# Values by the seven-product scheme, and two projection chains interleaved step by step, in a sandwich of attention and gated feed-forward

## The chip, the cores and the metric

The kernel runs on one core of a Trainium2 chip. The metric is the device time of one execution in microseconds (us); the time before is 1585.0 us, the median of three runs (1584.58 to 1585.37). One further execution was profiled. In the text TensorE is PE in the profile's letters (PEld is its weight load), VectorE is DVE, ScalarE is ACT, GpSimd is POOL and SyncE is SP, which here only issues transfers.

## The reference, cut to what matters

The input x has 8 batches of 512 rows of 256 numbers, in 32-bit floats. There are 16 heads of 64 numbers each.

```python
x = x + _layernorm(attention(_layernorm(x)))
x = x + _layernorm(feed_forward(_layernorm(x)))

# attention, per batch
q, k, v = x @ w_q, *split(x @ w_kv)          # 256 -> 1024 each, then 16 heads
q = l2norm(q) * exp(scale);  k = l2norm(k)   # per head and row
out = softmax(q k^T) v                       # 512 x 512 scores per head
return out @ w_out + b_out                   # 1024 -> 256

# feed-forward
h = silu((x @ w1) * s1) * ((x @ w2) * s2)    # 256 -> 1024
h = gelu((h @ h1) * hs1);  h = gelu((h @ h2) * hs2)   # 1024 -> 1024, weights -1, 0, 1
return (h @ w3) * s3                         # 1024 -> 256
```

## The kernel before, in words

The attention of all 8 batches runs first and the feed-forward of all 8 after it. Only the attention part is touched by the change; the feed-forward part starts when the last batch's attention is done.

**Units.** The attention goes by head pairs: a batch has 8 pairs, and a pair of a batch is a unit, so there are 64 units. Pairs 0 to 3 use the first half of the q, k and v columns (half 0, 512 columns), pairs 4 to 7 the second (half 1). A unit's own work is: `scores` (L738: eight products of 64 rows by 512, called s), the exponentials on ACT (L749, tile e, scaled by the key norms kn), their sum over the key blocks on DVE (`summed`, L772, tile es), `values` (L792: products of e with v, called po), the copy of po to oT on ACT (L888), and for every second unit the row sums pd on PE (L816) with their inverse: copied to d on ACT (L830), folded by an SP transfer (L858) to a small tile, inverted on DVE (L878), stored and spread by two more SP transfers (L864, L869), and multiplied into oT on DVE (L898).

**The order of the work.** PE does its work in the order in which the code adds it. For unit k that is: values of k, row sums, the work put in the odd slot 2k+1, scores of unit k+1, the work put in the even slot 2k, and then values of k+1. What is beside a unit is named in the table `BESIDE`, one string for each pair of a batch: c is one step of a query or key projection, v a step of the value projection, q and k the query and key norms (odd slot; all others even), m the key norms' transposes, o an output projection of 128 rows of the batch before, x the layer norm and transposes of the next batch's input, t the sums of token quarters, l a load. Steps of half 1 for the batch itself stand in the first strings, steps for the next batch in the later ones. The other engines and SP do their work in an order that a planner (`Steps.issue`) writes out beforehand from estimated costs; each engine and the SP queue then runs its list in that order, whatever the actual times are.

**The projections.** For batch 0 all projections are plain products (`qk_step`, `v_step`). For batches 1 to 7 queries and keys of a half go by a chain of seven products of quarters (Strassen's scheme in Winograd's form, `qk_chain`), L539: the weights are cut in four 128 by 256 quarters, the transposed input aT in four 128 by 256 quarters, sums of them are made on DVE (the weights' once, in `qk_weight_sums`, tile wsum; the input's once per batch in `token_sums`, tile tsum), and each product is two matmuls of 256 columns instead of the eight quarter products of the plain way. Products 1, 6, 7 and 4 are added up in one bank of PSUM (g1), products 5 and 3 in another (g2), product 2 in a third (g3). In between, ACT copies the intermediate sums out (`kept`, L560) or DVE adds them to what was kept (`added`, L570), and ACT squares the result for the norms (`squared`, L578). A product that adds to g1 has to wait until the sum before it is copied or added. The values go by the plain way in all batches: `v_step` is two matmuls of 512 columns (L407, tile vp) and one copy on ACT (L721), four steps for a half.

**The norms.** `norms_step` multiplies the squares with a matrix of ones (L627, pn), copies the sums on ACT to a tile nd (L651), and for queries folds them by SP (L633), inverts them on POOL, stores them (L674) and spreads them (L641, tile spread) for a multiplication into qT on DVE (L684). For keys `key_norms` transposes nd on PE (L698, pk) and POOL takes the power to kn. The tiles d and nd come from one pool of two buffers (`sqp`, tag "sq").

**PSUM.** Seven banks are dealt out in turn to all of this (`wbank`), an eighth holds po. A chain holds g1 and g2 over several steps.

**Weight work.** In the DVE's free time the kernel checks that the feed-forward weights are what the fast way presumes (`looked_at`: an SP load into tile w, L1083; `marked` L1090 and `gathered` L1095 on DVE, 512 columns each) and makes the sums of quarters of h1 and h2 (`weight_sums`, L1127, stored to DRAM by L1131). Tile w has two buffers.

Of the kernel before, what the change touches and what calls it, by code (L numbers as in the profile page):

```python
# [17 lines left out]
P = 128  # L18
# [121 lines left out]
def tile_fast(  # L140
# [143 lines left out]
    wp = attn_scope.enter_context(tc.tile_pool(name="wp", bufs=2))  # L284
# [115 lines left out]
    def projected(key, b, t, w, c0):  # L400
# [3 lines left out]
        def run():  # L404
# [11 lines left out]
            "pe", 1.72, run, reads=[(("aT", b), t)], writes=[(key, 0)],  # L416
# [55 lines left out]
    wsum = qksum.tile([P, 4, 3, 2 * P], F32, name="wsum")  # L472
    HS = S // 2

    def quarter(which, hf, k):
        w = wq_sb if which == "q" else wk_sb
        if k[0] == "A" or k == "S3":
            i, j = (1, 0) if k == "S3" else (int(k[1]) - 1, int(k[2]) - 1)
            return w[:, j, hf * HALF + i * HS : hf * HALF + (i + 1) * HS]
        return wsum[:, "qk".index(which) * 2 + hf, "S1 S2 S4".split().index(k), :]  # L480

    def qk_weight_sums(which, hf):
# [35 lines left out]
    def qk_chain(b, hf, which):  # L518
# [3 lines left out]
        to, sq, t = (which + "T", b, hf), ("spread", *n), ("tsum", b)  # L522
        g, tags = [("g1", *n), ("g2", *n), ("g3", *n)], {}

        def product(k, a, x, bank, fresh, last=False):
# [4 lines left out]
            def run():  # L530
# [7 lines left out]
                for o in range(2):  # L538
                    nc.tensor.matmul(  # L539
                        T[key][:, o, :], lhsT=w[:, ts(o, P)], rhs=rhs,  # L540
                        start=(fresh and o == 0), stop=True, skip_group_check=True,
                    )
# [10 lines left out]
        def part(i, k):  # L553
            return T[to][:, 2 * i : 2 * i + 2, ts(k, HS)]

        def kept(i, k, key, first=False):
            def run():
                if first:
                    tile_of(qkTp, [P, HP, S], which + "T", to)
# [4 lines left out]
                takes=[(which + "T", 2, to)] if first else (),  # L564
# [9 lines left out]
        def squared(i):  # L574
# [6 lines left out]

            steps.add(
# [14 lines left out]
        def fourth():  # L597
            added(0, 1, product(3, "S4", "B22", 1, False, last=True))

# [3 lines left out]
        def sixth():  # L603
            added(0, 0, product(2, "A12", "B21", 2, True, last=True))
            squared(0)
# [5 lines left out]
        return [first, second, third, fourth, sixth, fifth, seventh]  # L611
# [170 lines left out]
    def values(b, p, jb):  # L782
# [4 lines left out]
        def products():  # L787
# [13 lines left out]
            "pe", 0.86, products, reads=[(e, 0), (e, 1), (v, jb)], writes=[(po, 0)],  # L801
# [100 lines left out]
    def out_proj(b, t, pairs=(0, NP), tail=False):  # L902
# [72 lines left out]
        "c c v c c c c v c x x x x",  # L975
        "k o m o t",
        "c c o c c c c o c",
        "q v v l",
        "c c v c c c c v c",
        "k v",  # L980
        "c c m c c c c v c",
# [7 lines left out]
    def chains(b, hf):  # L989

        for w in "qk":
            yield from (lambda k=k, w=w: link(b, hf, w, k) for k in range(7))

    links = {}

    def link(b, hf, w, k):
        if k == 0:
            links[w] = qk_chain(b, hf, w)
# [9 lines left out]
    def beside():  # L1008
# [4 lines left out]
        c = [s for b, hf in c for s in ((b, s) for s in chains(b, hf))]  # L1013
        n = [(b, lambda b=b, hf=hf, w=w: norms_step(b, hf, w)) for b, hf in n for w in "qk"]
        m = [(b, lambda b=b, hf=hf: key_norms(b, hf)) for b, hf in m]
        v = [(b, lambda b=b, hf=hf, t=t: v_step(b, hf, t)) for b, hf in v for t in range(NT)]
        x = [(b, lambda b=b, t=t: norm_in(b, "a", t, ("xres", b))) for b in range(1, B) for t in range(NT)]
        o = [(b, lambda b=b, t=t: out_proj(b, t)) for b in range(B - 1) for t in range(NT)]
        for b in range(B):
            for p, some in enumerate(BESIDE):  # L1020
                for k in some.split():
                    later = p > 1 and (p > 3 or k in "cqkm")
# [12 lines left out]
                    elif (b + 1 < B) if later else b:  # L1035
                        yield b * NP + p, k, {"c": c, "q": n, "k": n, "m": m, "v": v}[k].pop(0)[1]
        assert not (c or n or m or v or x or o)
# [31 lines left out]
    loose = const.tile([P, S], I32, name="loose")  # L1069
# [7 lines left out]
    def looked_at(n, k, rows_of, after):  # L1077
# [3 lines left out]
        def load():  # L1081
            dst = tile_of(wp, [P, HID], "w", w)
            nc.sync.dma_start(  # L1083
                dst if len(rows_of.shape) == 2 else dst.rearrange("p (c n) -> p c n", n=D), rows_of
            )

        def marked(i):

            a, y = T[w][:, ts(i, S)], ("y", n, k, i)
            nc.vector.scalar_tensor_tensor(  # L1090
                tile_of(sump, [P, S], "y", y, bufs=1), a, 0.0, a, ALU.is_equal, ALU.add
            )

        def gathered(i):
# [6 lines left out]
            "sync", 0.1, load, lag=9.0, writes=[(w, 0), (w, 1)], takes=[("wrows", 2, w)], earliest=after  # L1101
        )
        for i in range(2):
            y = ("y", n, k, i)
            steps.add(
                "dve", 0.72, lambda i=i: marked(i), reads=[(w, i)], writes=[(y, 0)],
# [1134 lines left out]
```

## Time and profile before

| | |
|---|---|
| median of the runs | 1585.0 us |
| the profiled execution's own time | 1584.32 us |
| its span, first to last instruction | 1582.5 us |
| PE / DVE / ACT / POOL busy, share of the span | 99 / 67 / 58 / 31% |
| attention, until the last output projection | about 979 us |
| one batch of the attention in the middle (577.54 to 697.60 us) | 120.06 us |
| in it: PE / DVE / ACT / POOL busy | 120.06 / 62.22 / 69.67 / 26.58 us |
| granted TensorE clock, mean | 0.998 |

The shares say which engine is full, and the chain that ended last says whether the time follows from it. The table of a batch is read by stretches: each stretch shows the PE's busy time beside its length. A 32-bit matmul is shown as two records, so a chain product of two matmuls has four.

### The profile page before, as it was taken

What the parts mean: (1) busy time and instruction counts of PE and PEld (TensorE: products, weight loads), DVE (VectorE), ACT (ScalarE), POOL (GpSimd) and SP (SyncE); (2) the same over time, 40 slices, a digit from 0 to 9 for tenths busy, and PEclk for the clock granted to TensorE, in tenths of its full rate; (3) what the DMA queues carried; (4) which work ended last, traced back from release to release, by engine and by line L of the source; (5) the groups of instructions that cost most, each with busy time, mean ns of one, the idle gap of its engine ahead of it and who ended that gap; (6) DMA issues with size and microseconds to landing.
All of it is one profiled execution on the core that took longest, in us unless ns stands there. A gap on an engine that the chain in (4) does not pass through costs nothing.

```text
span 1582.5 us, 19689 instructions
## 1 busy us (share of the span) xinstructions
PE 1564.5 (99%) x7208; PEld 996.6 (63%) x7208; DVE 1059.5 (67%) x1772; ACT 917.6 (58%) x1543; POOL 486.6 (31%) x354
## 2 busy tenths in 40 slices
PE   9999999999999999999999999999999999999997
PEld 4344554554554554554554546788888888888886
DVE  4577776786654553554544557869877886879686
ACT  4666556556556556555555553666466636655662
POOL 4212122122221221321221211554165235625451
PEclk9999999999999999999999999999999999999999
DMA  6233433342220220220221313344324523451540
GB/s 178 65 97 102 120 82 109 121 115 76 54 62 15 58 65 15 58 62 18 58 64 43 85 38 88 111 142 156 121 80 133 171 69 107 146 152 49 160 133 29
DMA packets 77829, 142.66 MB, mean 90 GB/s; under 512 B 18844, under 2 KB 34460, under 8 KB 73628
## 3 DMA queue, kind: packets, MB, share of 16 engines
q1 hardware_dynamic: 58140, 78.40, 17.9%
q0 software_dynamic: 18880, 61.87, 12.5%
q8 instruction: 58, 0.95, 0.3%
q10 hardware_dynamic: 704, 1.05, 0.2%
q14 instruction: 47, 0.39, 0.1%
HBM read 123.49 MB, written 17.29 MB: 89 GB/s over the span
## 4 chain that ended last, share of the span: by engine, by line
PE 96%; DVE 2%; DMA 1%; ACT 0%; issue 0%; POOL 0%; SPq 0%; DVEq 0%
PE g L1494 26%; PE s L738 15%; PE po L792 14%; PE pa L914 7%; PE vp L407 7%; PE p L1420 6%; PE g_q L539 5%; PE g_k L539 5%; PE py L1608 4%; PE pd L816 2%; PE pn_q L627 1%; PE pn_k L627 1%; PE kp L433 1%; PE qp L433 1%; PE pk L698 0%; DMA spread_q<-nq 0%
## 5 line engine op out<-in xcount | busy, mean ns | idle before, releaser
L749 ACT ACTIVATE e<-s,kn 128x512 f32<-128x512 f32 x512 | 306.7, 702 | 96.6 <-PE s L738 96.6
L738 PE MATMUL s<-qT,kT 64*128 64x512 f32 x1024 | 237.1, 602 | 0.0
L1494 PE MATMUL g<-h,wb_S 128*128 128x512 f32 x1024 | 234.3, 389 | 0.0
L792 PE MATMUL po<-e,v 128*64 128x512 f32 x1024 | 233.9, 598 | 0.0
L1494 PEld LDWEIGHTS g<-h,wb_S 128*128 128x128 f32 x1024 | 192.0, 188 | 39.8
L738 PEld LDWEIGHTS s<-qT,kT 64*128 64x128 f32 x1024 | 93.6, 186 | 143.2 <-issue 125.7
L1494 PE MATMUL g<-h,wb_A 128*128 128x512 f32 x768 | 176.4, 389 | 0.0
L314 POOL TENSOR_TENSOR kn<-kn,neghalf 128x32 f32<-128x32 f32 x16 | 87.5, 5468 | 285.8 <-DVE kn L702 285.8
L772 DVE TENSOR_TENSOR es<-es,e 128x1024 f32<-128x1024 f32 x128 | 156.8, 1225 | 24.9 <-ACT e L749 14.0
L1494 PEld LDWEIGHTS g<-h,wb_A 128*128 128x128 f32 x768 | 144.0, 188 | 29.7
L792 PEld LDWEIGHTS po<-e,v 128*64 128x64 f32 x1024 | 69.4, 136 | 139.7 <-issue 131.1
L1312 DVE TENSOR_TENSOR h<-C,h 128x512 fp32r<-128x512 f32 x112 | 129.4, 1211 | 3.9 <-ACT h L1302 3.8
L314 POOL TENSOR_TENSOR nf_q<-nf_q,neghalf 128x32 f32<-128x32 f32 x16 | 87.3, 5456 | 144.9 <-DVE nf_q L661 144.9
L772 DVE TENSOR_TENSOR es<-e,e 128x1024 f32<-128x1024 f32 x64 | 78.3, 1224 | 72.2 <-ACT e L749 71.9
L1312 DVE TENSOR_TENSOR h<-B,h 128x512 fp32r<-128x512 f32 x112 | 107.8, 1001 | 27.1 <-ACT h L1302 26.7
L407 PE MATMUL vp<-wv_sb,aT 128*128 128x512 f32 x256 | 120.6, 599 | 0.0
L914 PE MATMUL pa<-wo_sb,oT 128*128 128x256 f32 x512 | 116.5, 381 | 0.0
L1550 POOL TENSOR_TENSOR B<-B,B 128x512 f32<-128x512 f32 x64 | 102.0, 1621 | 38.9 <-DVE B L1451 34.0
L914 PEld LDWEIGHTS pa<-wo_sb,oT 128*128 128x128 f32 x512 | 95.8, 190 | 20.0 <-ACT e L749 6.1
L888 ACT COPY oT<-po 128x512 f32<-128x512 f32 x64 | 37.4, 584 | 120.2 <-PE po L792 118.2
L878 DVE RECIPROCAL fold<-fold 128x16 f32<-128x16 f32 x31 | 7.8, 252 | 147.0 <-DMA fold<-d 147.0
L1550 POOL TENSOR_TENSOR C<-C,C 128x512 f32<-128x512 f32 x64 | 94.0, 1495 | 27.7 <-DVE h L1312 27.2
(170 smaller groups left out, 2320.8 us busy)
## 6 DMA issues: line engine op xcount, KB each, us to landing
wb_S<-s POOLq DMA_DIRECT2D x32, 1024.0 KB, 5.1
spread_q<-nq SPq DMA_DIRECT2D x32, 512.0 KB
rden<-r SPq DMA_DIRECT2D x62, 256.0 KB
wb_A<-in_h1T_dram POOLq DMA_DIRECT2D x12, 1024.0 KB, 5.6
wb_A<-in_h2T_dram POOLq DMA_DIRECT2D x12, 1024.0 KB, 5.6
s<-w SPq DMA_DIRECT2D x32, 256.0 KB
w<-in_h1T_dram SPq DMA_DIRECT2D x8, 512.0 KB
x<-xres SPq DMA_DIRECT2D x32, 128.0 KB
```

The costliest lines, as they stand in the source:

```text
L314: nc.gpsimd.tensor_tensor(d, d, neghalf.to_broadcast([P, n]), ALU.pow)
L407: nc.tensor.matmul(pm, lhsT=T["aT", b][:, c, ts(t, P)], rhs=w[:, c, c0 : c0 + HALF], start=(c == 0), stop=(c == ND - 1),)
L539: nc.tensor.matmul(T[key][:, o, :], lhsT=w[:, ts(o, P)], rhs=rhs, start=(fresh and o == 0), stop=True, skip_group_check=True,)
L738: nc.tensor.matmul(tile_of(ps_w, [P, S], tags[h], ss[h]), lhsT=T[kT][hp, j, ts(jb, P)], rhs=T[qT][hp, j, :], start=True, stop=True,)
L749: nc.scalar.activation(T[e][:, h, :], T[ss[h]], AF.Exp, scale=T["kn", b, hf][:, jb, 2 * j + h : 2 * j + h + 1],)
L772: nc.vector.tensor_tensor(T[t], T["e", b, p, 0] if jb == 1 else T[t], T["e", b, p, jb], ALU.add)
L792: nc.tensor.matmul(T[po][h * DH : (h + 1) * DH, :], lhsT=T[v][:, jb, c0 : c0 + DH], rhs=T[e][:, h, :], start=(jb == 0), stop=(jb == NT - 1),)
L914: nc.tensor.matmul(T[pm], lhsT=T["oT", b, p][:, ts(t, P)], rhs=wo_sb[:, p, :], start=(p == 0), stop=(p == NP - 1),)
L1312: lambda: nc.vector.tensor_tensor(T[h][:, 1, c, :], T[raw][:, c, :], T[h][:, 0, c, :], ALU.subtract),
L1420: nc.tensor.matmul(T[ps[k]], lhsT=(w1r, w2r)[k][c][:, ts(o, P)], rhs=row_halves(b, i)[0][:, c, :], start=(c == 0 and i == 0), stop=(c == N ...
L1494: nc.tensor.matmul(T[to[o]], lhsT=T[w][:, c, ts(o, P)], rhs=T[h][:, i, c, :], start=(first and c == 0 and i == 0), stop=(c == NQ - 1 and i ...
L1550: lambda: (nc.gpsimd if T_ENGINE == "pool" else nc.vector).tensor_tensor(T[dst][:, c, :], T[x][:, c, :], T[y][:, c, :], ALU.subtract),
```

## The change

The values of batches 1 to 7 go by the same chain of seven products as queries and keys: `qkv_chain` takes "v" too, with the input as the stationary and the weights as the moving operand, and squares nothing for it. Its weight sums are added (`qkv_weight_sums`, six groups instead of four), and they stand behind the value projections of batch 0 in the code, since one of them overwrites a quarter of the weights.

Two chains now run beside each other, a step of the one and a step of the other in turn. In the strings of `BESIDE`, c is a step of a query chain, d of a key chain, v of a value chain. Pair 0 has key and value chain of the batch's half 1, pair 2 query and key chain of the next batch's half 0 with two output projections among their first steps, pair 6 the query chain of half 1 and the value chain of half 0 of the next batch. Pairs 3, 4, 5 and 7 have only norms and the transposes of m. Both norms of half 0 stand in pair 3 (the key norms were in pair 5), and m of half 0 in pair 4 (was in pair 6). Within a chain the addition of the fourth product and the first squares come later: the order is first, second, third, sixth, fifth, fourth, seventh.

The weight work is cut in tiles of half a row (two loads of 256 KB each instead of one of 512 KB for h1 and h2), its DVE instructions are 256 columns wide instead of 512, twice as many, and its stores are 128 KB instead of 256 KB, 64 instead of 32. Tile w has one buffer instead of two. The work is put in at every fourth slot from slot 8.

```diff
-    wp = attn_scope.enter_context(tc.tile_pool(name="wp", bufs=2))
+    wp = attn_scope.enter_context(tc.tile_pool(name="wp", bufs=1))
...
-    wsum = qksum.tile([P, 4, 3, 2 * P], F32, name="wsum")
+    wsum = qksum.tile([P, 6, 3, 2 * P], F32, name="wsum")
...
                 for o in range(2):
+                    x_, y = (rhs, w) if which == "v" else (w, rhs)
                     nc.tensor.matmul(
-                        T[key][:, o, :], lhsT=w[:, ts(o, P)], rhs=rhs,
+                        T[key][:, o, :], lhsT=x_[:, ts(o, P)], rhs=y,
                         start=(fresh and o == 0), stop=True, skip_group_check=True,
                     )
...
         def part(i, k):
+            if which == "v":
+                i, k = k, i
             return T[to][:, 2 * i : 2 * i + 2, ts(k, HS)]
...
         def fourth():
             added(0, 1, product(3, "S4", "B22", 1, False, last=True))
+            squared(0)
...
         def sixth():
             added(0, 0, product(2, "A12", "B21", 2, True, last=True))
-            squared(0)
...
-        return [first, second, third, fourth, sixth, fifth, seventh]
+        return [first, second, third, sixth, fifth, fourth, seventh]
...
     BESIDE = (
-        "c c v c c c c v c x x x x",
+        "d v d v d v d v d v d v d v x x x x",
         "k o m o t",
-        "c c o c c c c o c",
-        "q v v l",
-        "c c v c c c c v c",
-        "k v",
-        "c c m c c c c v c",
+        "c d o c d o c d c d c d c d c d",
+        "q k l",
+        "m",
+        "",
+        "c v c v c v c v c v c v c v",
         "q",
     )
...
-        v = [(b, lambda b=b, hf=hf, t=t: v_step(b, hf, t)) for b, hf in v for t in range(NT)]
+        v = [(b, lambda b=b, hf=hf, k=k: link(b, hf, "v", k)) for b, hf in v for k in range(7)]
...
-    loose = const.tile([P, S], I32, name="loose")
+    STRIP = 256
+    loose = const.tile([P, STRIP], I32, name="loose")
...
         steps.add(
-            "sync", 0.1, load, lag=9.0, writes=[(w, 0), (w, 1)], takes=[("wrows", 2, w)], earliest=after
-        )
-        for i in range(2):
+            "sync", 0.1 * len(loads), load, lag=9.0, writes=[(w, i) for i in range(4)],
+            takes=[("wrows", 1, w)], earliest=after,
+        )
+        for i in range(4):
...
     for i, work in enumerate(weight_work()):
-        at(8 + 10 * i if i < NH else 56 + 4 * i, work)
+        at(8 + 4 * i, work)
...
-    for hf in range(2):
-        for w in "qk":
-            qk_weight_sums(w, hf)
     norms_step(0, 1, "q")
     for t in range(NT):
         v_step(0, 1, t)
...
+    for hf in range(2):
+        for w in "qkv":
+            qkv_weight_sums(w, hf)
```

In the changed program PE's list has 16 instead of 128 matmuls of the value projection's form and 196 new ones of 256 columns; full-array work stands between scores and values at 37 places instead of 51. On ACT, the copy of nd for the keys' half 0 stands between the first and the second exponential of pair 4.

## The prediction

> **What bounds the kernel now.** I read the page's first part and its chain first, then the chain of one batch in the middle, then a table by stretches, and last the ACT, SP and DVE timelines beside it.
>
> ```profile
> PE 1564.5 (99%) x7208; PEld 996.6 (63%) x7208; DVE 1059.5 (67%) x1772; ACT 917.6 (58%) x1543; POOL 486.6 (31%) x354
> PE 96%; DVE 2%; DMA 1%; ACT 0%; issue 0%; POOL 0%; SPq 0%; DVEq 0%
> ```
>
> The chain that ended last is PE for 96% of the span: the time is the sum of PE's work, and other engines count only where PE waits. The chain of one batch shows the pieces (start, us, what):
>
> ```profile
> 588.39 1.93 PE g_k L539 x8
> 590.31 1.72 PE vp L407 x4
> 592.03 3.45 PE g_k L539 x16
> 595.48 1.72 PE vp L407 x4
> 597.20 0.86 PE g_k L539 x4
> 598.06 3.58 PE po L792 x16
> ...
> 607.14 1.91 PE vp L407 x4
> 609.05 3.58 PE po L792 x16
> ...
> 630.15 3.63 PE s L738 x16
> 633.78 3.58 PE po L792 x16
> ```
>
> A value step (two matmuls, four records) is 1.72 us; four chain products (sixteen records) are 3.45, so one is 0.8625. The first full-array piece after scores is dearer: 1.93 instead of 1.725 for two products, 1.91 instead of 1.72 for a value step, about 0.195. And po costs 3.58 whether full-array work or scores stand before it: entering a block of full-array work costs 0.195, leaving it nothing more than scores to po costs anyway. In the table by stretches (length, then busy time of PE, PEld, DVE, ACT, POOL) the middle batches have no PE idle time, but for one:
>
> ```profile
> 336.04:456.11 120.07, 120.07 (x546) 62.66 (x545) 79.36 (x135) 69.70 (x117) 26.92 (x12) 1.00 0.27 72
> 456.11:577.54 121.43, 120.33 (x545) 62.58 (x545) 62.21 (x106) 69.56 (x117) 26.39 (x12) 1.00 0.18 45
> 577.54:697.60 120.06, 120.06 (x545) 62.66 (x545) 62.22 (x107) 69.67 (x117) 26.58 (x12) 1.00 0.18 46
> ```
>
> The slower one, in the chain:
>
> ```profile
> 467.40 6.83 DMA spread_q<-nq
> ...
> 474.94 1.89 DVE kT L570 x3
> ...
> 476.87 1.13 PE g_k L539 x4
> ```
>
> The query norms' spread of half 0 landed late; the DVE's multiplication waits for it ahead of three chain additions, and PE waits for these. That cost 121.43 - 120.06 = 1.37 us.
>
> **The change, part by part.** The sum is against the profiled execution (1584.32 us, of which 1.8 lie around its span of 1582.5); the median of the runs, 1585.0, is 0.7 above it.
>
> *Values.* Per batch 8 steps of 1.72 (13.76) go and 14 products of 0.8625 (12.075) come: -1.685, in 7 batches -11.8 us. All of it lies on PE's path.
>
> A rule of the Trainium skill speaks against this ("TensorE: Matmul & The Clock Gate", section "Back-to-back issue gap": in a stream of weight loads and matmuls the spacing is set by both). The chain matmuls have 256 columns for each weight load, the value steps 512, so there are 14 x 28 - 7 x 32 = 168 more load records, of 0.19 each by the row of L407's loads; were they all exposed, the sum would be -11.8 + 31.9 = +20.1. The rows of L539 already pair them so, and 3.45 / 16 = 0.216 is longer than 0.19, so the sum goes by the row.
>
> *Blocks.* Full-array work stands between scores and values at 37 places instead of 51 (pairs 3 and 5 lose theirs; pair 4 keeps one for m alone): 14 x 0.195 = -2.7 us. Output projections, transposes and norms keep their number; where they stand costs the same 3.45 and 0.86.
>
> *The chain's own waits.* With a second chain between, g1 is added to again after four products instead of two: three others, 2.6 us, cover a copy of 0.59 or an addition of 0.69. PE's idle time before L539 in the rows is 0.2 + 0.8 (batch 0) and 1.1 (the late spread). Half 0's spread now lands under pairs 5 and 6, before the next chain; half 1's still lands in pair 0's chains. On DVE its multiplication stands behind the first chain's addition of product 7; in the last three batches it stands ahead of the second's. Bounds: -2.4 (0.99 in batch 0, 1.37 in the middle) to +1.37 x 7 = +9.6, if every batch met one such late spread. I take -1.7: batch 0's are the same products with cover, and half of a late spread.
>
> *Norms of half 0 side by side.* This adds a wait. In pair 3 d, nd of the queries and nd of the keys want two buffers at once, so the keys' copy waits for d's fold transfer, and it stands between the first and second exponentials of pair 4. Behind it seven exponentials are queued, and po of pair 4 waits for them, with no full-array work between. The nearest row is the unit at 630.15, which is bare too; here are its fold and exponentials, from the timelines of SP, ACT and DVE:
>
> ```profile
> 629.97 0.58 SPq L858 DMA_DIRECT2D fold<-d  x1
> 631.30 4.73 ACT L749 ACTIVATE e<-s,kn 128x512 f32<-128x512 f32 x8 [0.50 <-PE s L738]
> 631.85 0.25 DVE L878 RECIPROCAL fold<-fold 128x16 f32<-128x16 f32 x1 [8.98 <-DMA fold<-d]
> ```
>
> The exponentials end at 636.03; the fourth key block of po begins at 633.78 + 0.75 x 3.58 = 636.46: 0.43 us of cover, against one copy more of 0.59, so 0.16 to 0.25 with a handover. In pair 3 a second norm (0.86) lies between d and the scores, so the fold that here lands 1.9 us after its issue, 0.55 after the first exponential began, lands before the copy wants it. Bounds: 0 (hidden) and 0.25 + 0.86 a batch, if the fold comes a whole norm later: 7.8 in seven. I take 0.23 x 7 = +1.6, from the nearest row.
>
> *Other engines, at no cost.* DVE gets 42 additions of 0.69 (29 us), about 4.1 a batch. Weight work: 88 + 32 instructions of 0.69 become 176 + 64 of 256 columns; at 0.42 (the row of L509, two inputs of 256 columns) 101 instead of 83 us, +18. Cover: DVE is busy 62 to 89 of 120 us a batch. If it were gone, an addition late by one 0.42 instruction would still lie inside the 2.6 us. Eight more weight sums at the start (3.4 us at 0.42) stand before the first es, where DVE had 3.55 us idle waiting for exponentials. ACT's four copies for a half of v stay four of 0.59. Bounds for all of this: 0 and, if the start's sums are wholly exposed, +3.4; I take 0. SP: 16 more loads (0.53 each) and 32 more stores (0.32), some 19 us of issuing, in a queue that waited 317 us for d alone; but a queue that is blocked holds back the folds behind it, and that is a rival below. POOL's keys' power of half 0 (5.4 us) comes about two pairs earlier and is wanted by pair 0 of the next batch: covered by pairs 6 and 7. The feed-forward's lists are in the same order; it and the end of the attention are taken as they were.
>
> *Sum.* -11.8 - 2.7 - 1.7 + 1.6 = -14.6: 1584.3 - 14.6 = 1569.7 profiled, 1570.4 as a median; I say 1570.5. One batch of the middle: 120.06 - 1.69 - 0.39 + 0.23 = 118.2.
>
> The Trainium skill's "Perfetto Trace Analysis" (section "Identifying the Most-Contended Engine") warns against reading matmul busy time and would have the weight loads' share looked at. Here that is 63%, and by it PE would have room, so that removed products might give nothing and the time stay at 1585. The chain of waits, not the 99%, carries my argument.
>
> **The rivals.**
>
> *A: bare pairs wait for ACT.* Pairs 4, 5 and 7 have nothing to hide the exponentials, and pair 4 has the extra copy. For it: 0.43 us of cover. Against it: the bare unit at 633.78 has no idle time, though it too had d and one nd copied. If pair 4 loses the bound of 1.1 a batch, 6 more than taken: 1576.5.
>
> *B: late spreads or additions in the double chains.* Six additions of 0.69 fall due within six products of 0.86, and the spread's multiplications among them. For it: the 1.37 at 467. Against: only once in seven batches. At 1.37 in each, +9.6 instead of -1.7: 1581.8.
>
> *C, slower: the SP queue is blocked.* Tile w has one buffer, so each load waits in the queue until four stores of the tile before have landed, and stores wait for low-priority DVE sums; SP waited up to 14.6 us for one such sum (L1131 waiting for DVE w). A fold queued behind comes late, the keys' copy waits for it, and with it seven exponentials and po. It decides from 14.2 us of lost time, about 2.8 in each of the five batches that I expect to have weight work. At 5 us each, 25 instead of 1.6: 1594. Against it: before, spans from a fold's issue to its inverse were 1.9 us with weight work about, and the changed list puts that fold ahead of the sums' stores.
>
> *D: no change.* The PE's products are not what sets the time, or A and B together give the gain back. The chain speaks against it: 1585.
>
> **How the numbers follow.** The forecast (1567 to 1574): 0.70; A: 0.14; B: 0.07; C: 0.05; D: 0.04. The measurement can tell about 0.2%, 3.2 us, from no change. Faster: forecast, A and nearly all of B with a part of D, 0.92; same 0.03; slower 0.05. Range: the low end has no new wait and all old ones gone, 1584.3 - 14.5 - 2.4 = 1567.4 without the median's 0.7, so 1567; the high end holds A and the lower part of B: 1578.
>
> **What would show it.** Right: batches of 118 to 118.5 us; vp (L407 before) shrinks to 32 records and new g_v records come at 0.216 each in the chain; 14 fewer pieces at 1.91 or 1.93. The copy: an idle stretch of PE before po of pair 4, put down to ACT e, of 0.2 us. A shows there with 1 us or more, B as PE waiting before L543 for DVE, C as ACT waiting for fold or SP waiting for stores. The forecast is wrong if PE has idle time of over 1 us a batch anywhere in the middle batches, or if g_v products take longer than 0.8625.

## The result and the profile after

The changed kernel takes 1577.3 us (median of five runs, 1575.8 to 1578.4) beside 1584.6 for the kernel before on the same chip: ratio 0.9956, 95% interval 0.9945 to 0.9967. That is 7.3 us less, where I had forecast 14.5 less. The profiled execution took 1577.85 us, its span 1576.0 (before 1582.5).

The page of the changed kernel, its busy times and the shares of the chain that ended last:

```profile
PE 1556.3 (99%) x7376; PEld 1034.1 (66%) x7376; DVE 1103.6 (70%) x1942; ACT 913.2 (58%) x1543; POOL 484.4 (31%) x354
PE 93%; DVE 4%; DMA 2%; issue 0%; ACT 0%; SPq 0%; POOL 0%; DVEq 0%; POOLq 0%; ACTq 0%
```

PE is "99% busy" as before, yet its share of the chain fell from 96 to 93%, and DVE and DMA, which had 3% together, have 6%. The busy share hardly shows this: batch 1 below is 1.29 us longer than an undisturbed batch, and 1.03 of that is drawn as busy, 0.26 as idle. The chain shows it.

The table by stretches cuts the span at the first scores of each batch (length, then busy time of PE, PEld, DVE, ACT, POOL); these are batches 0, 1, 4, 5 and 7:

```profile
55.32:146.75 91.43, 91.43 (x438) 44.82 (x437) 63.37 (x102) 62.17 (x105) 16.60 (x4) 1.00 0.29 77
146.75:266.24 119.49, 119.23 (x572) 67.99 (x568) 84.50 (x162) 68.99 (x116) 26.36 (x12) 1.00 0.31 85
...
502.71:623.53 120.82, 119.24 (x572) 67.98 (x568) 84.46 (x160) 69.09 (x116) 26.32 (x12) 1.00 0.25 67
623.53:741.73 118.20, 118.20 (x572) 67.86 (x568) 66.61 (x112) 69.05 (x116) 26.51 (x12) 1.00 0.19 46
...
859.94:973.23 113.29, 108.69 (x497) 58.29 (x493) 65.37 (x107) 55.73 (x95) 17.39 (x13) 0.98 0.18 48
```

Against the same cut of the kernel before:

| stretch | before | after | difference |
|---|---|---|---|
| up to the first scores | 55.22 | 55.32 | +0.10 |
| batch 0 | 93.23 | 91.43 | -1.80 |
| batch 1 | 120.07 | 119.49 | -0.58 |
| batch 2 | 120.06 | 118.21 | -1.85 |
| batch 3 (in it the late spread before) | 121.44 | 118.26 | -3.18 |
| batch 4 | 120.06 | 120.82 | +0.76 |
| batches 5 and 6, each | 120.06, 120.07 | 118.20, 118.21 | -1.86 |
| batch 7, to the first feed-forward product | 109.50 | 113.29 | +3.79 |
| feed-forward | 602.81 | 602.75 | -0.06 |

Undisturbed batches are the 118.2 of the forecast. The rest was lost in batch 1, batch 4 and the last batch (and 0.6 in batch 0). Pair by pair, all of it lies between the scores of pair 5 and those of pair 7. The chain of an undisturbed batch, first products of a double chain, then pairs 4 and 5:

```profile
634.45 1.06 PE g_k L543 x4
635.51 0.86 PE g_v L543 x4
...
700.57 3.86 PE po L802 x16
...
708.65 3.58 PE po L802 x16
712.23 1.00 PE pd L827 x8
```

A value product takes the 0.86 of a query or key product, the first one after scores 1.06, and po of pair 4 takes 3.86 instead of 3.58. In the changed kernel pd stands at L827, es at L782 and the multiplication by the inverses at L909; `r<-fold` is the store of the inverses, `rden<-r` their spread. The same place in batch 4:

```profile
573.40 1.04 PE pd L827 x8
...
577.33 3.75 DMA r<-fold
...
581.76 4.27 DMA rden<-r
...
586.05 0.69 DVE oT L909
...
587.49 0.35 DVE y L1103
...
590.12 1.15 DVE es L782
...
593.97 1.05 PE pd L827 x4
```

Here is the new wait. The row sums pd of pairs 4 and 5 need the sum es of pair 5. es stands on DVE behind the multiplication of oT by the inverses of pairs 2 and 3, and those were folded, inverted, stored (3.75 us) and spread (4.27) meanwhile. Behind the multiplication DVE also took six instructions of weight work (y, loose). In the last batch the fold was late:

```profile
917.66 1.00 PE pd L827 x8
...
921.91 3.25 DMA fold<-d
...
927.51 4.02 DMA rden<-r
...
931.62 1.29 DVE oT L909 x2
...
936.76 1.05 PE pd L827 x4
937.82 5.33 PE s L748 x16
```

The data of this fold were copied by 919.3, but SP issued it only at 921.91: its queue stood 3.4 us at a reload of rows (L1063) that waited for their store. The last line is a second loss. After 2.69 us without work PE takes 5.33 us for scores that take 3.63 elsewhere: the granted clock is 0.50 between 938 and 941 us. So 1.7 of what the last batch lost is no wait for es, but a slow clock after it. In batch 4, after 1.58 us without work, the clock stayed at 1.00 and the scores took 3.63.

How tight it had become is seen on DVE in an undisturbed batch (start, length, idle time before and what ended it); first the kernel before:

```profile
711.65 1.23 DVE L772 TENSOR_TENSOR es<-es,e 128x1024 f32<-128x1024 f32 x1 [0.73 <-ACT e L749]
```

In the chain of the kernel before, the row sums that take it:

```profile
721.71 0.99 PE pd L816 x8
```

DVE in the changed kernel:

```profile
704.83 0.69 DVE L909 TENSOR_TENSOR oT<-oT,rden 128x512 f32<-128x512 f32 x1
...
707.97 1.23 DVE L782 TENSOR_TENSOR es<-e,e 128x1024 f32<-128x1024 f32 x1 [1.71 <-ACT e L759]
709.30 2.55 DVE L782 TENSOR_TENSOR es<-es,e 128x1024 f32<-128x1024 f32 x2
```

Before, the last es of pair 5 ended at 712.88 and pd started at 721.71: 8.8 us to spare, because a chain and value steps stood in pairs 4 and 5. After, it ended at 711.85 and pd started at 712.23: 0.4 to spare, and 1.7 more that DVE spends waiting for the exponentials. So about 2.0 us of delay are free, and each one beyond is PE's.

That margin predicts the losses. From the fold's issue to the multiplication an undisturbed batch takes 8.93 us (695.89 to 704.83). Batch 1 took 12.29 (3.36 late; 3.36 - 2.0 = 1.4, lost 1.3). Batch 3 took 10.30 (1.37 late, nothing lost). Batch 4 took 10.98 and had 2.6 of weight work before es (2.05 + 2.6 - 2.0 = 2.7, lost 2.6). With 4.8 in the last batch (3.79 and the 1.04 that its half-1 values and one block should have saved; 1.7 of it by the clock) and 0.6 in batch 0, 9.3 us were lost; without them the span would be 1566.7.

### The profile page after: what moved, and what is told of

Its sections match the earlier page's. It is cut to its first block, busy times and chain, and to the rows that moved or that the text cites. A ratio compares the mean times of both kernels' runs of the same rounds, so it can differ in the third digit from the quotient of the medians.

```text
span 1576.0 us, 20323 instructions
## 1 busy us (share of the span) xinstructions
PE 1556.3 (99%) x7376; PEld 1034.1 (66%) x7376; DVE 1103.6 (70%) x1942; ACT 913.2 (58%) x1543; POOL 484.4 (31%) x354
## 4 chain that ended last, share of the span: by engine, by line
PE 93%; DVE 4%; DMA 2%; issue 0%; ACT 0%; SPq 0%; POOL 0%; DVEq 0%; POOLq 0%; ACTq 0%
PE g L1522 26%; PE s L748 14%; PE po L802 13%; PE pa L925 7%; PE p L1448 6%; PE g_q L543 5%; PE g_v L543 5%; PE g_k L543 5%; PE py L1636 3%; PE pd L827 2%; PE vp L407 1%; PE kp L433 1%; PE qp L433 1%; DMA rden<-r 1%; PE pn_q L637 1%; PE pn_k L637 1%
## 5 line engine op out<-in xcount | busy, mean ns | idle before, releaser
L782 DVE TENSOR_TENSOR es<-es,e 128x1024 f32<-128x1024 f32 x128 | 156.7, 1225 | 17.5 <-ACT e L759 6.7
L782 DVE TENSOR_TENSOR es<-e,e 128x1024 f32<-128x1024 f32 x64 | 78.2, 1222 | 62.4 <-ACT e L759 62.2
L314 POOL TENSOR_TENSOR ors<-ors,neghalf 128x1 f32<-128x1 f32 x32 | 19.3, 605 | 262.2 <-DVE kn L712 164.7
L1569 DVE TENSOR_TENSOR C<-g,C 128x512 f32<-128x512 f32 x96 | 65.3, 687 | 45.1 <-PE g L1522 45.1
L1547 ACT ACTIVATE C<-C,hs_sb 128x512 f32<-128x512 f32 x96 | 68.6, 722 | 47.7 <-DVE C L1569 47.5
```

The source lines that it names most:

```text
L314: nc.gpsimd.tensor_tensor(d, d, neghalf.to_broadcast([P, n]), ALU.pow)
L782: nc.vector.tensor_tensor(T[t], T["e", b, p, 0] if jb == 1 else T[t], T["e", b, p, jb], ALU.add)
L1547: nc.scalar.activation(T[dst][:, o, :], x, AF.Gelu, scale=s[:, f : f + 1])
```

## The experiments

Theory 1: DVE stands in its list at an instruction whose data come from outside, the multiplication by the inverses, and the sums es behind it, which pairs 4 and 5 no longer cover, reach PE late. Theory 2: the bare pairs wait for the exponentials or for the weight work, whatever stands before es. The medians of the kernel before in the four sets of runs were 1584.2, 1584.3, 1584.3 and 1583.9. The intervals of the ratios are about 2 us to either side, so where two runs differ by less than 4 us, what is said rests on the stretches of their profiles, each of one execution. In these profiles too a long wait can end in a granted clock of 0.50: for 3.4 us in batch 2 of the first run, in batch 0 of the order undone alone and in batch 1 with the multiplication on POOL, for 6.8 in batch 2 of the products as cover. Up to half of such a stretch is lost besides the wait.

**The multiplication behind es.**

```diff
-        steps.add("sync", 0.1, stored, reads=[(f, 0)], writes=[(("rd", b, p), 0)], lag=1.5)
+        steps.add("sync", 0.1, stored, reads=[(f, 0)], writes=[(("rd", b, p), 0)], lag=5.5)
...
-            writes=[(r, c) for c in range(2)], takes=[("rden", 1, r)], lag=4.0,
+            writes=[(r, c) for c in range(2)], takes=[("rden", 1, r)], lag=5.0,
```

> The changed kernel with one thing edited: the planner is told that the inverses' store takes 5.5 us instead of 1.5 to land and their spread 5.0 instead of 4.0, so that DVE's list has the multiplication of oT by the inverses of pairs 2 and 3 behind the sums es of pair 5 (and not between those of pair 4 and 5). Theory 1 (the lost time is PE waiting in pairs 4 and 5 for es, and es is late because DVE stands in order at a multiplication whose inverses have not landed; 1.30 us in batch 1, 2.62 in batch 4, 4.81 in the last, 8.7 in all): the row sums of pairs 4 and 5 start on time in every batch, 1577.3 - 8.7 = 1568.6, between 1567 and 1571. Theory 2 (es of pair 5 is late because the exponentials or the weight work are, whatever stands before it): the same stretches stay, 1576 to 1579. If the multiplications stand in front of other work instead, pairs 6 and 7 or the tail lose what pairs 4 and 5 win.

Measured: 1574.8 us (1573.1 to 1579.6), ratio 0.9945 (0.9932 to 0.9957). Batch 2, batch 4 and the last batch by stretches:

```profile
264.43:388.42 123.99, 120.65 (x573) 68.22 (x569) 84.91 (x162) 69.12 (x116) 26.73 (x12) 0.99 0.32 87
...
506.63:626.28 119.65, 119.25 (x573) 67.99 (x569) 82.17 (x155) 69.05 (x116) 26.92 (x12) 1.00 0.25 68
...
862.70:971.19 108.49, 106.30 (x496) 57.78 (x493) 65.37 (x107) 55.77 (x95) 16.95 (x13) 1.00 0.19 51
```

The last batch got all of its 4.8 back, batch 1 nearly its 1.3 (118.4) and batch 4 half of its 2.6. The place is right. But batch 2, clean in the changed kernel, took 124.0. There SP and DVE say (in this order):

```profile
349.77 1.23 SPq L1096 DMA_DIRECT2D w_(1, 1)_2789<-in_h2T_dram  x2
351.10 1.27 SPq L651 DMA_DIRECT2D spread_q<-nq  x2
```

```profile
361.66 1.90 DVE L694 TENSOR_TENSOR qT<-qT,spread_q 128x512 f32<-128x512 f32 x3 [6.38 <-DMA spread_q<-nq]
```

The spread of the query norms was issued behind two weight loads of 256 KB and arrived 10 us later (about 7 at this place in other batches). DVE stood 6.4 us at its multiplication, and everything behind, sums and then chain additions, came late. The mechanism has a second instruction.

**Row sums later.** In `units`, `inverted_two` is called after the scores of the next pair.

```diff
-        elif p % 2:
-            inverted_two(b, p - 1)
...
         for n in ahead:
             for jb in range(NT):
                 scores(*n, jb)
+        if p % 2 and (b, p // 2) != (B - 1, HP - 1):
+            inverted_two(b, p - 1)
```

> The changed kernel with one thing edited: in PE's list the row sums pd stand behind the scores of the next pair, not ahead of them (the four pairs at the very end excepted), which gives es 3.6 us more and makes everything that hangs on the row sums 3.6 us later. Theory 1: stretches shorter than 3.6 us vanish (1.30 in batch 1, 2.62 in batch 4), the last batch keeps 1.2 of 4.8, if the multiplications, 3.6 us later, do not stand in front of another sum: 1577.3 - 3.9 - 3.6 = 1569.8, between 1568 and 1573. Theory 2 (exponentials late): the same gain could come, since es has more time whatever it waits for; this run tells only whether the place of the row sums is where the time is lost. If it is lost elsewhere: 1577.

Measured: 1596.9 (1595.2 to 1597.9), far outside. The stretches at pairs 4 and 5 are gone, but the best of the middle batches takes 119.3, and with the inverses 3.6 us later, chains wait instead (the chain in batch 2):

```profile
288.40 9.55 DMA spread_q<-nq
...
298.65 0.68 DVE v L578
...
299.99 2.08 PE g_k L543 x4
```

**Products as cover.** The value chain of the next batch's half 0 goes to the bare pairs.

```diff
-        "m",
-        "",
-        "c v c v c v c v c v c v c v",
+        "m v v v",
+        "v v v v",
+        "c c c c c c c",
```

> The changed kernel with one thing edited: the seven value products of the next batch's half 0 stand in pairs 4 (three) and 5 (four) instead of pair 6, where the query chain is then alone. Pairs 4 and 5 are bare no longer, in all batches but the last. Theory 1 (the row sums of pairs 4 and 5 had 0.31 us to spare and now have 3.5 and more): batches 1 and 4 lose their 1.30 and 2.62; one full-array block more in seven batches costs 7 x 0.195 = 1.4; the last batch keeps its 4.8: 1577.3 - 3.9 + 1.4 = 1574.8, between 1573.5 and 1577. If the lone query chain waits for its own additions as one of before did (0.2 to 1.4 a batch), 1 to 9 us more. Theory 2: batches 1 and 4 stay at 119.5 and 120.8 plus 0.2.

Measured: 1594.9 (1594.1 to 1596.8): also wrong. An undisturbed batch takes 120.6. The lone chains wait for their own copies and additions: in batch 4 two additions of the value chain stand on DVE behind es of the pair, and the last product of pair 5 starts after them, at 619.1. And batch 2 takes 128.6, again by the spread:

```profile
357.07 9.95 DMA spread_q<-nq
...
367.12 2.50 DVE qT L694 x4
...
374.77 0.69 DVE v L578
...
375.51 2.07 PE g_v L543 x4
```

Chain products do not cover a late DVE, since they need DVE's additions themselves. The plain value steps that stood there before needed none: their one copy was on ACT.

**Without the weight work,** in the changed kernel, in the changed kernel with the multiplication behind es, and in the kernel before.

```diff
-    for i, work in enumerate(weight_work()):
-        at(8 + 4 * i, work)
...
-            src = sums_dram[l, int(k[1])]
+            src = rows_[:, :NQ, ts(int(k[1]) % 2, HALF)]
```

> The changed kernel without the weight work: the feed-forward weights are not looked at, the sums of quarters of h1 and h2 are not made, and the feed-forward takes quarters of h1 and h2 in place of them (same sizes, another result). Nothing else is edited. Theory 1 (two things make the multiplication late: the inverses' store shares the queue with the weight work's stores and loads, 3.6 us instead of 1.4 in batches 1 and 4, and weight work on DVE; in the last batch it is the fold, 3.25 us, with no weight work about): batches 1 and 4 take 118.2, the last batch keeps its 4.8, so 1577.3 - 3.9 = 1573.4, between 1572.5 and 1574.5. Theory 3 (all of it is the weight work): 1568.6. Theory 2 (bare pairs wait for the exponentials): 1577.

> The changed kernel without the weight work (weights not looked at, no sums of quarters; the feed-forward takes quarters of h1 and h2 in their place) and with the multiplications by the inverses behind the sums of pair 5 (store said to take 5.5 us, spread 5.0). If the lost time is the DVE's in-order wait and the weight work's transfers and instructions, and nothing else, this is what the working forecast for the products, blocks and norms: 1584.3 - 14.6 = 1569.7 profiled, median 1570; batches of 118.2 throughout and about 83.0 from the last batch's first scores to its last. If the multiplications moved behind cost time of their own at their new place (as in batch 2 with the weight work, 5.8 us), more than 1573.4, the median without the weight work alone.

> The kernel before without the weight work (weights not looked at, no sums of quarters; the feed-forward takes quarters of h1 and h2 in their place). Taking it out of the changed kernel gave 3.9 us. If that price is of the new layout (row sums with 0.31 us to spare where there were 8.8), it is worth only the late spread here: 1584.2 - 1.4 = 1582.8, and every batch of the middle takes 120.06. If the weight work costs its DVE and queue time anywhere, about 4: 1580.3.

Measured: 1573.4 (1571.6 to 1573.8), ratio 0.9934 (0.9921 to 0.9947), as expected; 1568.6 (1568.5 to 1569.4), ratio 0.9904 (0.9889 to 0.9919), 1.4 below the 1570 expected; and 1584.5 (1583.4 to 1585.3), ratio 1.0000 (0.9991 to 1.0009). The last batch of the first and of the second:

```profile
855.66:967.18 111.52, 107.03 (x496) 57.78 (x493) 65.35 (x107) 55.72 (x95) 17.40 (x13) 1.00 0.18 50
```

```profile
855.36:963.85 108.49, 106.31 (x496) 57.78 (x493) 65.34 (x107) 55.75 (x95) 16.95 (x13) 1.00 0.19 51
```

In both, batches 1 to 6 take 118.2 (one 118.5) and batch 0 90.9 instead of 91.4. So the weight work costs the changed kernel 3.9 us by the medians, 4.5 by batches 0, 1 and 4 of the profiles, and the kernel before nothing that the medians show. What it does not cause is the last batch's wait: 3.0 of the 4.8 are still lost without it, and this time the clock stayed at 1.00. The place of the multiplication takes that wait away. With both, the span is 1566.7, which is what the losses above left.

**Which part of the weight work.** One run keeps the transfers without DVE's instructions, one the instructions (on a tile that stands still) without the transfers, with all lists as they were.

```diff
...
-                lambda: nc.vector.tensor_tensor(part(into), part(x), part(y), op),
+                lambda: None,
```

```diff
-            dst = tile_of(wp, [P, HID], "w", w)
...
+            T[w] = still
...
-                lambda: nc.sync.dma_start(sums_dram[n, j][:, k, ts(c, STRIP)], part(into)),
+                lambda: None,
```

> The changed kernel without the DVE instructions of the weight work (weights not looked at, the sums not made), but with all its loads and stores, from SP, at the places that the planner gave them with the instructions counted: every list is otherwise the changed kernel's. The feed-forward takes what was stored, quarters instead of sums. If the weight work costs its 3.9 us by its transfers alone (inverses' stores of 3.6 us and spreads of 7 to 10 behind 256 KB and 128 KB), the stretches stay, with the 2.6 us of instructions in front of es in batch 4 gone: 1575 to 1577. If by DVE's instructions alone: 1573.4. A store cannot wait for a late sum here, so that a gain of a part of it may also be SP's queue being free.

> The changed kernel with the DVE instructions of the weight work, on one tile that is never loaded, and without its loads and stores; every list is otherwise the changed kernel's. The feed-forward takes quarters of h1 and h2. If the transfers are what costs: 1573.4, batches 1 and 4 at 118.2 or near. If the DVE's instructions: 1576 to 1577.5. In between, each has its share, and the two runs should add up to the 3.9 of leaving out both.

Measured: 1574.8 (1573.6 to 1575.1) with transfers only, 1574.5 (1573.5 to 1575.7) with instructions only. Batches 1 and 4, first of the transfers, then of the instructions:

```profile
147.00:265.90 118.90, 118.90 (x572) 67.99 (x569) 66.46 (x112) 69.11 (x116) 26.12 (x12) 1.00 0.32 86
502.47:620.68 118.21, 118.21 (x573) 67.86 (x569) 66.37 (x112) 69.12 (x116) 26.10 (x12) 1.00 0.26 68
```

```profile
146.59:264.79 118.20, 118.20 (x572) 67.86 (x568) 85.20 (x162) 69.04 (x116) 26.55 (x12) 1.00 0.18 46
501.20:620.31 119.11, 119.11 (x573) 67.98 (x569) 84.26 (x160) 69.03 (x116) 26.32 (x12) 1.00 0.19 46
```

Neither alone is the culprit. With transfers alone the inverses' store still takes 3.6 to 3.8 us and the multiplication is 2.8 and 1.9 late, which costs 0.7 and nothing; with the instructions alone the multiplication is on time and 2.6 of weight work cost 0.9. Alone they cost 0.7 and 0.9 in these two batches, together 3.9: both eat the same 2 us of margin, and a part that fits into it is free. Batch 0's 0.6 goes with the instructions: the stretch is 91.4 with them alone, 90.9 with the transfers alone.

**The weight work's transfers from POOL,** alone, and with the multiplication behind es.

```diff
-                nc.sync.dma_start(
+                nc.gpsimd.dma_start(
...
-            "sync", 0.1 * len(loads), load, lag=9.0, writes=[(w, i) for i in range(4)],
+            "pool", 0.9 * len(loads), load, lag=9.0, writes=[(w, i) for i in range(4)],
...
-                "sync", 0.1,
-                lambda: nc.sync.dma_start(sums_dram[n, j][:, k, ts(c, STRIP)], part(into)),
+                "pool", 0.9,
+                lambda: nc.gpsimd.dma_start(sums_dram[n, j][:, k, ts(c, STRIP)], part(into)),
```

> The changed kernel with all its work, the transfers of the weight work alone (two loads and four stores a tile) issued by POOL in place of SP, the planner told 0.9 us of POOL for each. Theory 1a (the weight work hurts through the SP queue: an inverses' store or spread stands behind loads and stores, or behind a store that waits for a DVE sum): batches 1 and 4 take 118.2, the last keeps its 4.8, 1573.4 as without the weight work. Theory 1b (it hurts through the DMA engines that both queues share, or through DVE's instructions): 1576 to 1578, inverses' stores of 3 us and more stay. A loss is possible where the powers on POOL come late behind a store that waits: keys' norms wanted by the exponentials, above 1578.

> All of the changed kernel's work, with both edits: the weight work's transfers issued by POOL, and the multiplications by the inverses behind the sums of pair 5 (store said to take 5.5 us, spread 5.0). If theory 1a holds, about 1570 as with the weight work left out; if 1b, the 1574.8 of the second edit alone, or between. It would be faster than both kernels.

Measured: 1581.7 alone (1577.7 to 1585.2), slower than the change as it was; 1570.9 with both (1569.4 to 1571.2), ratio 0.9913 (0.9899 to 0.9926), faster than both kernels. Alone it is no cure, which speaks against theory 1a: the inverses' store still took 1.4 to 3.6 us in the batches with weight work, and a spread 9.6. Chain of batch 2 with the queue alone:

```profile
278.24 9.63 DMA spread_q<-nq
...
287.96 0.06 DVE qT L694
...
288.57 0.69 DVE v L578
...
289.31 1.13 PE g_v L543 x4
```

The Trainium skill's "DMA: Bandwidth & Descriptors" (section "Queues, rings and completion order") says that each DMA engine serves its queue rows in turn, a packet at a time. The store of up to 3.6 us is in line with it: in these runs another queue did not give a small transfer the engines to itself.

**The spread's multiplication later too.** To both edits, the planner is told 11.0 us for the spread of the norms (`lag=7.5` becomes 11.0).

> The changed kernel with all its work and three edits: the weight work's transfers issued by POOL, the multiplications by the inverses planned 5.0 us later, and the spread of the norms said to take 11.0 us instead of 7.5, so that DVE stands later at the multiplication by the query norms. In the run with the first two edits a spread of 8.7 us (632.17) let DVE stand 2.0 us in front of a chain's additions, and two batches took 119.1 and 119.3. If that is all that is left: 1570.9 - 2.0 = 1569, near 1568.6 without the weight work. If the multiplication goes in front of something else, 1571 or more.

Measured: 1569.4 (1569.2 to 1570.1), ratio 0.9911 (0.9898 to 0.9925), with all of the work done; batches 1 and 4 are 118.21 and the last 108.50. It is within a microsecond of the run that leaves the weight work out (1568.6). So the three edits together give back nearly all that was lost, with DVE meeting the two multiplications later in its list. The share of each is not shown: the third was not run alone, its 1.5 us lie within the intervals, and why the queue helps behind the first edit (1574.8 to 1570.9) though it hurts alone was not taken apart.

**The same two edits on the kernel before.**

> The kernel before with the two edits that gave 1570.9 on the changed one: the weight work's transfers issued by POOL (32 loads and 32 stores fewer in SP's queue, its tiles of before kept), and the multiplications by the inverses planned 5.0 us later. If the edits only take away what the changed kernel had made tight, nothing is to be had here but the late spread of one batch: 1583 to 1585, and the products' gain stands alone as 1570.9 against this. If they are good for either kernel, 1578 or less.

Measured: 1591.5 (1586.3 to 1595.4), ratio 1.0041 (1.0026 to 1.0056): worse. In its profile batches 1 and 2 take 121.7 and 122.6, PE waiting for additions of the key chain in pair 4. The profiled execution took 1586.7; what the longer ones lost besides is not shown. The edits are no general gain; the changed kernel's advantage stands.

**The multiplication on POOL.**

```diff
-            nc.vector.tensor_tensor(T[o], T[o], x, ALU.mult)
+            nc.gpsimd.tensor_tensor(T[o], T[o], x, ALU.mult)
...
-        steps.add("dve", 0.69, run, reads=[(r, c) for c in range(2)], writes=[(o, 0)])
+        steps.add("pool", 1.5, run, reads=[(r, c) for c in range(2)], writes=[(o, 0)])
```

> The changed kernel with one thing edited: the multiplications of oT by the inverses (64 of 0.69 us) run on POOL instead of DVE, the planner told 1.5 us each. DVE stands at no inverses any more, and no sum es is queued behind them. Theory 1: the stretches of pairs 4 and 5 go wholly, whatever the weight work's transfers do to the inverses: 1577.3 - 8.7 = 1568.6, between 1567 and 1572. If what hurts is that es is late on its own account (exponentials, weight work on DVE), 1575 to 1578. POOL's own queue can be the new place: a power of a norm (5.4 us) behind a multiplication that waits; then PE waits before scores or po for the exponentials, and the end, where the multiplication stands on the path, loses about a microsecond.

Measured: 1582.9 (1580.0 to 1586.5); theory 1 as I had put it expected 1568.6. Batch 1 takes 126.6. DVE there:

```profile
234.35 1.25 DVE L677 TENSOR_SCALAR nf_q<-nf_q,escale 128x32 f32<-128x32 f32 x1 [2.66 <-POOL nf_q L314]
235.52 0.41 DVE L1103 SCALAR_TENSOR_TENSOR y_(3, 0)_0_1885<-w_(3, 0)_1817 128x256 f32<-128x256 f32 x1
235.96 1.38 DVE L1108 SCALAR_TENSOR_TENSOR loose<-y_(3, 0)_0_1885,loose 128x256 int32<-128x256 int32 x1
```

DVE no longer stands at the inverses; it stands at nf_q, which waits for POOL's power, then does weight work, then es. Of the 8.4 us that the batch is longer, 1.7 are again scores at half the clock (5.33 us at 244.54). In batch 4 DVE stands at the spread. It is not one instruction: whichever in DVE's list waits for the outside takes the place.

**The order undone.** Values by seven products, but query and key chains one after the other as before, value products dealt out beside three of the four chains; alone, and with the two edits.

```diff
-        "d v d v d v d v d v d v d v x x x x",
+        "c v c v c v c v c v c v c v x x x x",
...
-        "c d o c d o c d c d c d c d c d",
-        "q k l",
-        "m",
-        "",
-        "c v c v c v c v c v c v c v",
+        "c c o c c c c o c",
+        "q l",
+        "c c v v c c v c c v c",
+        "k",
+        "c c m c v c c v c v c",
...
-        return [first, second, third, sixth, fifth, fourth, seventh]
+        return [first, second, third, fourth, sixth, fifth, seventh]
```

> The changed kernel with the order of the work beside the attention undone as far as the memory allows: values by seven products as changed, but the query and key chains one after the other as before, with value products dealt out beside the chains of pairs 0, 4 and 6, the key norms of half 0 back in pair 5 and m in pair 6, and a chain's own steps in the order of before. Pair 4 is bare no longer. Per batch 1.69 for the values and 0.20 for one block of full-array work, 118.2, if the chains do not wait for their own additions. Theory 1 (the order with bare pairs 3 to 5 made the row sums tight): the middle batches have no stretch of over 0.3, the last, bare in both, keeps 3 to 5: 1584.3 - 11.8 - 1.4 - 1.0 + 4 = 1574, between 1572 and 1577. If the weight work's smaller tiles cost their time in any order: 4 more. If single chains wait, as in the run with the value chain in pairs 4 and 5 (2.2 a batch), up to 15 more.

> The same order of work with the two edits besides (the weight work's transfers issued by POOL, the multiplications by the inverses planned 5.0 us later). If dealing out two chains beside each other gives nothing by itself, the same 1569 to 1571 as the changed kernel with the two edits (a batch of 118.2 in both: 0.20 more for a block, 0.28 less at po of pair 4). If it is worth the waits of single chains, this is slower by those.

Measured: 1585.3 (1583.3 to 1590.2) and 1585.4 (1581.9 to 1588.5), no gain over the kernel before. The row sums of pairs 4 and 5 have 7.6 us and more to spare again, as expected, but chains wait in most batches (119.0 to 120.4 in the first, an undisturbed one 118.7), and batch 0 takes 96.9 in the first. The same products bring 7 us with two chains side by side and nothing without. Which of the differences (order within a chain, partner, place of the norms) does it was not taken apart.

## Why the prediction was wrong

**Values, blocks.** Right. Eight steps of 1.72 became fourteen products of 0.8625; the undisturbed batch went from 120.06 to 118.20, 1.86 less, where the steps with the copy gave 1.85. The weight loads were hidden, as the row said.

**The chain's own waits.** Taken at -1.7, the bound -2.4 was right: with the disturbances taken out (the run without weight work and with the multiplication behind es), batch 0 and batch 3 have lost their old waits wholly. That run is 15.7 below the kernel before, against my sum of 14.6.

**Norms of half 0 side by side.** Right in place and nearly in size: po of pair 4 takes 0.28 longer, predicted 0.23.

**"Other engines, at no cost."** This is the step that failed: I put 0 with bounds 0 and +3.4, and it was 9.3 us in the profiled execution, 1.7 of them the slow clock behind the longest wait. I costed weight work by its instructions and the 2.6 us of cover of a chain's addition, and looked at how busy DVE is in a batch. I did not ask which of DVE's results PE needs next in the bare pairs. From the fold to the row sums of pairs 4 and 5 there are 8.9 us to the multiplication, 1.3 for it, and 3.8 for es, 14.0 of the 16.3 that two bare pairs give; the rest is the margin of 2.0 and gaps between instructions. All of these durations were in the trace of before (8.8 to 11.6 from the fold to the multiplication in pairs 2 and 3). "SP 0" had the queue in view, not that a store of 1.4 us takes 3.75 beside weight work. Even that stood there, in the batch of the one late spread that I took as a case by itself. The inverses' store, issued at 455.61 and 4.6 us behind a load of 512 KB, had taken 3.15 us, and DVE in the kernel before shows:

```profile
463.84 1.29 DVE L898 TENSOR_TENSOR oT<-oT,rden 128x512 f32<-128x512 f32 x2 [1.86 <-DMA rden<-r]
465.05 0.23 DVE L667 TENSOR_SCALAR nf_q<-nf_q,escale 128x32 f32<-128x32 f32 x1
```

It stood 1.86 us at the multiplication by the inverses, the query norms behind it went out late, and the spread of 467.40 then took no longer than others.

**Rival A** had the pairs and by luck the time (1576.5), and the wrong engine: ACT's exponentials were never late there by more than is in the 118.2. **Rival B** came true only in experiments, as the late spread. **Rival C** was right that the weight work's transfers reach PE, wrong on the price (3.9 with its instructions, not 25) and on the way: the fold was issued on time in batches 1 and 4, the inverses' store was slow, and from POOL's queue it was slow too. In the last batch a fold did stand behind a blocked queue, but without weight work. What I held against C was misread: 1.9 us from a fold's issue to its inverse is true of most, but the folds of pairs 2 and 3 took 2.3 to 3.5 in batches 1 to 6 of the kernel before. **Rival D** did not happen.

My own sign of failure, PE idle for more than 1 us in a batch, was seen in batch 4 (1.58) and in the last (2.69); in batch 1 only 0.26 of the 1.3 lost is drawn as idle.

## What to carry to other kernels

When work is taken out from between two stages of PE, list what it covered: not only the engine that feeds the next product, but every instruction that stands ahead of that one in the feeding engine's list, with the transfers those wait for. Work out the margin in microseconds (here from 8.8 to 0.4, or 2.0 with idle time) and compare it to how much the slowest transfer varies (here 2.3). Two disturbances that eat the same margin cost their sum less the margin together (in batch 4 nothing and 0.9 alone, 2.6 together), so running each alone understates both, and leaving out each in turn overstates them. Where a planner orders by fixed durations, try the slow value for what an in-order engine will stand at: it paid here, and together with the other queue it cost the kernel before 7 us.

## What was not expected of the hardware

A store of the folded inverses (128 rows of 16 numbers) takes 1.4 us alone and up to 3.75 beside loads and stores of the weight work; with those on another queue, still up to 3.6.

After 2.69 us without work in the last batch the granted TensorE clock was 0.50 for 3.4 us, and the scores cost 1.70 more; after 2.3 us in the same place of the run without weight work it stayed at 1.00.

While POOL multiplied 128 by 512 numbers (1.27 us), DVE instructions of 128 by 256 took 1.37 to 1.54 us in place of 0.42, and a small one 1.25 in place of 0.23. The Trainium skill's "SBUF — State Buffer" (section "SBUF: two separate sides") has a port pair that a DVE instruction with two inputs and a POOL instruction hold by turns, the whole instruction long; the rows with two inputs agree (the small one has one tensor and a number per partition). During POOL's powers (128 by 32, 5.4 us), the same DVE instructions took 0.42 to 0.43, so for the powers the length in the profile is not the time for which DVE is shut out.
